# The fifth chunk of the keys in six batches: nine full-array products replaced by fifteen block products in column halves of TensorE

## The chip, the cores and the metric

One core of a Trainium2 chip. The metric is the device time of one execution, in microseconds, as the median of several runs. The engines are TensorE (PE in the profile, its weight loads PEld), VectorE (DVE), ScalarE (ACT), GpSimd (POOL) and SyncE (SP, which issues DMAs here). Each engine runs its own instructions in order and waits for the others at semaphores.

## The reference

Cross attention in 16 batches. x has 100 rows of 640 a batch; the context has 718 text rows and 4 token rows of 384; 8 heads of 80.

```python
query = hidden_states @ Wq
keyt = enc @ Wk
valt = enc @ Wv
hs = _mha(query, keyt, valt)                  # softmax(q k^T / sqrt(80)) v
ca_q1 = einsum('btc,th->bch', ca, Wq_ca)[:, indices, :]
ca_hs1 = _mha(ca_q1, residual, residual)      # the tokens' first attention
ca_q2 = ca_hs1 @ Wq
ca_hs2 = _mha(ca_q2, ca @ Wk_ca, ca @ Wv_ca)  # and their second, over 4 tokens
out = (hs + ca_hs2) @ Wout + b_out + residual
```

All in fp32. The change touches `keyt`: 718 rows x 384 times 384 x 640, in every batch.

## The kernel before

**Fast products.** The products enc·Wk and enc·Wv are 3x3 by 3x2 block products: the context in thirds of its rows (u, KT = 240 columns each, two halves of KN = 120) and thirds of its 384 channels (c), the weights in thirds of the channels and two column groups (g). Plainly that takes 18 block products. `V_PLAN` (L95) lists 15: each entry is a bank ("A" to "E"), a form f (a sum of blocks of the context times a sum of blocks of the weights) and the output (u, g) that is to receive the bank's running sum after this product. A bank is not cleared between its products, so what it holds must be read before its next product writes. `enc_sums` (L481) makes the context's forms on POOL, `weight_sums` (L502) the weights', once at the start.

**Keys in five chunks.** kT has five chunks of 128 columns of Wk. The first four go through `Keys` (L453) as two pairs (a pair is a chunk's two groups g) with 15 forms each, K_PLAN (L113), banks A and B in `psumk` tiles and C, D, E in `psum1`. The fifth has no partner: `last_keys` (L685) does it plainly in `chunk_keys` (L662) with nine products of 128x128 weights and 240 columns, the raw blocks of `wk4` against the raw context, and two ACT copies (L678).

**PSUM.** Eight banks in three rings of two: `pair` (two banks each), `psumk`, `psum1`. A tile taken from a ring has the place of the tile two before it and waits until that one's last reader is done.

**One batch b**, in the order of the program from L1353: scores of b in three parts (L695; the second in `psumk` and `psum1`, the others in pairs), copied by ACT into st[0..2]; the column maximum (`larger`, `most`, `top`, class `Maximum` L785: DVE transpose, maximum, small maxima, spread, transpose back); `subtract(i)` on DVE and `exponential(i)` on ACT for the three parts; all the while TensorE does `Values(b)` and `Keys(b + 1)` in small steps (`vv.go`, `kk.go`); then `last_keys(b + 1)`, for some batches the output projection of two row chunks (`project_pair`, L1144), for odd b the queries of the next two batches; last the weighted values, `a_ps` (L1589), in two groups of four heads, and for the next but one batch `second_next.products()` (y_ps).

From L1352 on the order on every engine is that of the program (`manual_schedule`). So an instruction that waits holds up everything behind it on its engine.

**Odd batches from 3 to 13** make the queries in `Queries.make` (L607), products of 128x64 weights and 100 columns in the two column halves of TensorE (k = 0 and 64, partitions 0 and 64 of the output), after one plain product for qz with 200 columns. Its weights' and queries' sums are made on POOL (`sums`, L578), in the part of the next enc tile that is still free. `project_pair` falls in the batches where `last.b` = b − 1 is in `PAIRS` = {2, 5, 7, 10, 12}: so in 3, 11 and 13 among the odd ones. In 5, 7 and 9 (`parted`) the last token's product in `values2` (L991, POOL) stands behind the sums.

**The tokens' attention** of the next batch (`second`, class `Second` L854): `scores1` on POOL, `softmax1` (a second `Maximum`) on DVE, `exponentials1` on ACT; the products `z_ps` (L931) that use it come after the next batch's scores. `values2` makes hs2 on POOL, which DVE adds to hs after each group of `a_ps` (L1610). `keys(m_next)` (L842) writes the masks for `y_ps`, also on POOL.

Of the kernel before, what the change touches and what calls it, by code (L numbers as in the profile page):

```python
# [8 lines left out]
F32 = mybir.dt.float32  # L9
# [112 lines left out]
W_AT |= {f: 6 + i for i, f in enumerate((0, 1, 2, 6, 10, 11, 12, 3, 13))}  # L122
NF = len(V_PLAN)


@with_exitstack
def kernel(
# [124 lines left out]
    wk_sb = const.tile([P, NF, 2, P], F32, name="wk_sb")  # L252
    wk4 = const.tile([P, CC, P], F32, name="wk4")
    wq_sb = const.tile([P, HC, H], F32, name="wq_sb")
    kT = const.tile([P, HC, 3, KT], F32, name="kT")
# [100 lines left out]

    most = const.tile([P, ROWS], F32, name="most")
    nc.gpsimd.memset(most[96:, :], LOW)

# [121 lines left out]
    def enc_sums(enc):  # L481
# [3 lines left out]
        for out, left, right, op in (  # L485
# [14 lines left out]
            nc.gpsimd.tensor_tensor(out, left, right, op)  # L500

    def weight_sums(engine, w, late=None, there={}):  # L502


        at = lambda f: there.get(f, w[:, W_AT[f]])
        raw = lambda c, g: w[:, 2 * (c - 1) + g - 1]
        for f, left, right in (
            (0, raw(1, 2), raw(1, 1)),
            (11, raw(2, 2), raw(3, 2)),
            (12, raw(3, 2), raw(3, 1)),  # L510
            (5, raw(2, 2), raw(1, 2)),
            (7, raw(3, 2), at(5)),
            (13, raw(3, 1), at(7)),
            (1, raw(2, 1), raw(3, 1)),
            (3, raw(1, 1), at(7)),
            (6, raw(2, 1), raw(1, 1)),
            (10, raw(3, 1), raw(2, 2)),
            (2, raw(1, 1), raw(2, 2)),
            (14, raw(2, 1), raw(2, 2)),
        ):  # L520
# [38 lines left out]
    class Queries:  # L559
# [46 lines left out]

        def make(self, tiles, between):  # L607
            qp, qz = tiles
# [12 lines left out]
            def add(bank, g, m):  # L621
                nc.vector.tensor_tensor(q(g, m), full(bank), q(g, m), ALU.add)

            for ch in range(HC):
                for k in (0, 64):
                    nc.tensor.matmul(
                        full(f)[k : k + 64],
                        wq_sb[:, ch, 4 * P + k : 4 * P + k + 64],
                        self.xT[:, :, ch, :],
                        start=(ch == 0),  # L630
                        stop=(ch == HC - 1),
                        skip_group_check=True,
                    )
# [51 lines left out]
    def last_keys(b, enc):  # L685
# [6 lines left out]
        )  # L692


    def scores(b, g, tiles):  # L695
# [89 lines left out]
    class Maximum:  # L785


        def __init__(self, top, name, scalar=False):

            self.name, self.scalar = name, scalar  # L790
            self.step = self.steps(top)
            self.over = None
# [5 lines left out]
        def steps(self, top):  # L798
# [6 lines left out]
            for j in range(4):  # L805
                nc.vector.tensor_reduce(
                    side[:, j, :], quad[32 * j : 32 * j + 32, :].unsqueeze(2), AX.X, ALU.max
                )
            mx = small.tile([P, NB], F32, tag="mx", name=f"mx_{name}")
            scalar = self.scalar  # L810
            rows = 64 if scalar else 32
            for lo in range(0, 64 if scalar else P, 32):
# [5 lines left out]
                )  # L818
            yield
            spread = wide(f"spread_{name}").rearrange("p (b k) -> p b k", k=32)  # L820
# [33 lines left out]
    class Second:  # L854


        def __init__(self, b, xT, ca=None):
            self.b, self.xT = b, xT[:, b % 2]
            self.top = None
# [35 lines left out]
        def scores1(self, behind=None, tokens=range(T)):  # L895
            b, g = self.b, self.g
            e = e1[:S].rearrange("p (h s) -> p h s", h=NH)
            for t in tokens:
# [9 lines left out]
                if t:  # L908
                    nc.gpsimd.tensor_tensor(e, e, to, ALU.add)  # L909
                elif behind:  # L910
                    wait_for(first, behind)

        def softmax1(self, n=8):

            if not self.top:
                self.top = Maximum(e1, f"1_{self.b}", self.b - 2 in PAIRS)
            if self.top.over is not None:
                return
            self.top.go(n)
            if self.top.over is not None:  # L920
                nc.vector.tensor_tensor(e1[:S], e1[:S], self.top.over[:S], ALU.subtract)

# [99 lines left out]
    class Last:  # L1022
# [120 lines left out]

        def project_pair(self):  # L1144

# [27 lines left out]

            product(b1, [(one[:, :2], w(0, 0))], True)
            read(b1, 0, 0)
            product(b2, [(one[:, 2:4], w(1, 0)), (one[:, 4:], last(0))], True)
            read(b2, 0, 0)
# [3 lines left out]
            nc.gpsimd.tensor_tensor(two[:, :2], two[:, 2:4], two[:, :2], less)  # L1181
            nc.gpsimd.tensor_tensor(wout2[:, 0], wout2[:, 0], w(0, 0), less)
            product(b4, [(two[:, 2:4], wout2[:, 1])], True)
            product(b1, [(sum1, w(0, 1))], False)
# [168 lines left out]
    for b in range(B):  # L1353
# [38 lines left out]
        if b == 0:  # L1392
            enc_sums(enc)
            now.load(nc.gpsimd)
            now.softmax1()
        st.append(scores(b, 0, tiles))
        if b == 0:
# [46 lines left out]
        elif b + 1 < B:  # L1444
# [36 lines left out]
            if last.b in PAIRS:  # L1481
                last.sums()
            parted = b % 2 and b > 1 and last.b not in PAIRS
            now.values2(None, range(T - 1 if parted else T))
            vv.go(2)
# [15 lines left out]
            mixed = None  # L1501
            if b % 2 and b > 1:
                second_next, enc_next = loads()
                mixed = Queries(p + 1, xT_at[0], enc_next[0])
            if parted:
                mixed.sums()
                now.values2(None, range(T - 1, T))
            if b == 1:
# [12 lines left out]
            if last.b in PAIRS:  # L1521
                second.softmax1(3)
                last.project_pair()
                if last.b == max(PAIRS):
# [3 lines left out]
                    )  # L1528
            second.softmax1(3 if parted else 8)
        else:  # L1530
# [26 lines left out]
        if b % 2 and b + 1 < B:  # L1557
            xT, tiles = xT_at[0], queries_tiles(p + 1)
            if not mixed:
                for n in range(HC):  # L1560
                    queries(p + 1, xT, tiles, n)
            elif parted:
                mixed.make(tiles, second.softmax1)
            else:
                keys(m_next)
                mixed.sums()
                mixed.make(tiles, second.softmax1)
        if 0 < b < B - 2:
            if not mixed or parted:
                keys(m_next)  # L1570
            enc_sums(enc_next)
        if 0 < b < B - 1:
            second.exponentials1()

        mine.hs = hs = hs_sb
        hs2 = now.hs2
        for g in range(2):
# [6 lines left out]
            for h, i in order:  # L1584
                if b == B - 1 and h == NH - 1 and i == 0:
# [91 lines left out]
```

## Time and profile before

| what | value |
|---|---|
| median of 3 runs | 917.0 us (916.76 to 918.83) |
| the profiled execution, its own time | 916.04 us |
| its span, first to last instruction | 914.1 us |
| granted TensorE clock | 1.0 of full speed |
| DVE, ACT, POOL busy | 699.0, 434.2, 706.8 us |
| SP's hardware queue | 59.18 MB, 21.2% of 16 engines' span |

The page's chain of waits goes back from the last instruction, at each step to what released it. A row of a group reads: line, engine, operation, output and inputs by name, shapes, count, then busy time, mean ns of one, and the engine's idle time before them. For TensorE a shape 128\*64 128x200 is: 128 rows by 64 columns of weights, 200 columns streamed. An fp32 product is two records, and its modelled length overlaps the next; the spacing of the starts is what it takes. A row of the timeline is start and length (us), engine, line, operation, names, shape, count, and in brackets the idle time before it with what ended it. A row of the waits is who waited, for whom, total us, times, longest.

### The profile page before, as it was taken

Reading aid. Unit: us, or ns where it says so; the run is one execution under the profiler, and the core shown is the slowest. Engines: PE = TensorE matmul, PEld = TensorE weight load, DVE = VectorE, ACT = ScalarE, POOL = GpSimd, SP = SyncE. Lnnn points to the kernel's source line nnn. Section 1 sums busy time; section 2 is a strip of 40 time slices with the busy share of each in tenths; the row PEclk is TensorE's granted clock in tenths of the full one; section 3 lists DMA queues with packets and bytes.
Section 4 is the critical chain, followed back from the end, with each engine's and each line's share of the span. In section 5 each row is a group of like instructions: output and inputs, shape, how many; then the busy total and the mean of one; then the engine's idle time right before and its main releaser. Section 6 shows DMA issues by size and latency. Waiting matters only on the chain.

```text
span 914.1 us, 27711 instructions
## 1 busy us (share of the span) xinstructions
PE 908.2 (99%) x11962; PEld 762.8 (83%) x11962; DVE 699.0 (76%) x1126; ACT 434.2 (47%) x834; POOL 706.8 (77%) x672
## 2 busy tenths in 40 slices
PE   9999999999999999999999999999999999999998
PEld 6988889797797979888798787988879788797866
DVE  3669795989759897785967869679785897748883
ACT  2244543736337363652727436274741737427341
POOL 8577999787958879696896959958797697976623
PEclk9999999999999999999999999999999999999999
DMA  8822111131301212130121301103120031210111
GB/s 269 294 75 63 47 47 53 37 94 52 96 18 50 80 38 69 55 104 32 51 56 54 105 32 52 55 25 105 54 82 32 25 106 53 82 46 24 61 45 39
DMA packets 50582, 62.94 MB, mean 69 GB/s; under 512 B 13682, under 2 KB 37810, under 8 KB 50460
## 3 DMA queue, kind: packets, MB, share of 16 engines
q1 hardware_dynamic: 48812, 59.18, 21.2%
q8 instruction: 94, 1.54, 0.7%
q10 hardware_dynamic: 1024, 1.15, 0.4%
q0 software_dynamic: 624, 0.85, 0.3%
q14 instruction: 28, 0.23, 0.1%
HBM read 55.59 MB, written 5.57 MB: 67 GB/s over the span
## 4 chain that ended last, share of the span: by engine, by line
PE 96%; DVE 3%; ACT 0%; issue 0%; DVEq 0%
PE a_ps L1589 12%; PE s_ps L710 12%; PE v_psA L434 11%; PE v_psB L434 9%; PE k_psA L465 8%; PE k_psB L465 7%; PE kT_ps L667 6%; PE o_ps L1161 5%; PE v_psC L434 4%; PE k_psC L465 3%; PE q_ps L594 2%; PE q_ps L536 2%; PE v_psE L434 2%; PE v_psD L434 2%; PE v_ps L375 2%; PE q_psA L594 1%
## 5 line engine op out<-in xcount | busy, mean ns | idle before, releaser
L902 POOL TENSOR_TENSOR e<-ca,g 100x800 f32<-100x800 f32 x64 | 99.3, 1562 | 107.0 <-ACT kT L407 78.5
L500 POOL TENSOR_TENSOR enc<-enc 128x240 f32<-128x240 f32 x144 | 113.3, 797 | 14.7 <-DMA enc<-in_enct 7.5
L1375 DVE TENSOR_TENSOR st<-st,over 120x1600 f32<-120x1600 f32 x48 | 114.9, 2395 | 0.0
L1589 PEld LDWEIGHTS a_ps<-vs,st 120*36 120x36 f32 (+3 forms) x3072 | 109.3, 124 | 3.5 <-issue 3.4
L1589 PE MATMUL a_ps<-vs,st 120*36 120x81 f32 (+3 forms) x3072 | 111.7, 233 | 0.0
L434 PE MATMUL v_psA<-wv_sb,enc 128*120 128x320 f32 x352 | 109.3, 433 | 0.0
L1008 POOL TENSOR_TENSOR hs<-hs,hs 100x640 f32<-100x640 f32 x48 | 94.8, 1974 | 3.8
L1001 POOL TENSOR_TENSOR hs<-vb,p 100x640 f32<-100x640 f32 x64 | 91.1, 1434 | 8.4 <-issue 4.7
L465 PE MATMUL k_psA<-enc,wk_sb 128*128 128x240 f32 x384 | 95.3, 371 | 0.1
L909 POOL TENSOR_TENSOR e<-e,e 100x800 f32<-100x800 f32 x48 | 91.8, 1913 | 3.8
L434 PE MATMUL v_psB<-wv_sb,enc 128*120 128x320 f32 x296 | 91.8, 433 | 0.0
L1383 ACT ACTIVATE st<-st 120x1600 f32<-120x1600 f32 x48 | 73.9, 1539 | 32.3 <-DVE st L1375 31.8
L465 PEld LDWEIGHTS k_psA<-enc,wk_sb 128*128 128x128 f32 x384 | 71.5, 190 | 16.3 <-DVE wk_sb L522 0.5
L434 PEld LDWEIGHTS v_psA<-wv_sb,enc 128*120 128x120 f32 x352 | 64.2, 183 | 25.0 <-DVE vs L405 0.5
L1387 DVE TENSOR_TENSOR most<-most,st 120x800 f32<-120x800 f32 x64 | 66.3, 1036 | 15.9 <-ACT st L760 14.7
L465 PE MATMUL k_psB<-enc,wk_sb 128*128 128x240 f32 x320 | 78.0, 366 | 0.3 <-DVE sm L983 0.3
L710 PE MATMUL s_ps<-qp,kT 64*56 64x100 f32 (+1 forms) x3072 | 73.1, 248 | 0.0
L434 PEld LDWEIGHTS v_psB<-wv_sb,enc 128*120 128x120 f32 x296 | 54.1, 183 | 21.9 <-DVE vs L405 0.4
L710 PEld LDWEIGHTS s_ps<-qp,kT 64*56 64x56 f32 (+1 forms) x3072 | 66.9, 130 | 5.4 <-issue 4.2
L1076 ACT COPY hsT<-turned_hs 32x160 f32<-32x160 f32 (+7 forms) x244 | 67.7, 277 | 3.0
L465 PEld LDWEIGHTS k_psB<-enc,wk_sb 128*128 128x128 f32 x320 | 60.7, 190 | 8.6 <-issue 0.7
L766 ACT COPY st<-s_ps 120x800 f32<-120x800 f32 x64 | 49.8, 829 | 33.6 <-PE s_ps L710 33.6
(196 smaller groups left out, 1824.6 us busy)
## 6 DMA issues: line engine op xcount, KB each, us to landing
vb<-va_d SPq DMA_DIRECT2D x62, 250.0 KB
enc<-in_enct SPq DMA_DIRECT2D x30, 240.0 KB
enc<-in_enct SPq DMA_DIRECT2D x15, 360.0 KB
xT<-in_xt SPq DMA_DIRECT2D x8, 500.0 KB
rest<-in_enct SPq DMA_DIRECT2D x31, 120.0 KB
xn<-in_x SPq DMA_DIRECT2D x11, 320.0 KB
out<-xn SPq DMA_DIRECT2D x11, 320.0 KB
ca<-in_cas SPq DMA_DIRECT2D x16, 156.2 KB
```

Source lines behind the costliest of these rows:

```text
L434: nc.tensor.matmul(at[0][j][:KN, : H // 2], a_form(self.enc, f)[:, j * KN : (j + 1) * KN], wv_there.get(f, wv_sb[:, W_AT[f]]), start=first ...
L465: nc.tensor.matmul(at[:, i * KT : (i + 1) * KT], wk_sb[:, W_AT[f], i], a_form(self.enc, f), start=(first and i == 0), stop=last, skip_grou ...
L500: nc.gpsimd.tensor_tensor(out, left, right, op)
L710: nc.tensor.matmul(s_ps[at][k0:k1, cols], w, rhs, start=not begun & {(at, k) for k in range(k0, k1, 32)}, stop=last, skip_group_check=True,)
L902: first = nc.gpsimd.tensor_tensor(to, self.ca[:, t, :].unsqueeze(1).to_broadcast([S, NH, S]), g[:, :, t].unsqueeze(2).to_broadcast([S, NH, ...
L909: nc.gpsimd.tensor_tensor(e, e, to, ALU.add)
L1001: first = nc.gpsimd.tensor_tensor(to, self.vb[t][:S].rearrange("p (h d) -> p h d", h=NH), p2[:, :, t].unsqueeze(2).to_broadcast([S, NH, D] ...
L1008: nc.gpsimd.tensor_tensor(sums, sums, to, ALU.add)
L1076: nc.scalar.copy(self.hsT(r)[32 * m : 32 * m + 32, :, first - lo : end - lo], turned[32 * i : 32 * i + 32, :, m, first - at : end - at],)
L1375: return nc.vector.tensor_tensor(st[i], st[i], top.over[:KN].unsqueeze(1).to_broadcast([KN, 2, ROWS]), ALU.subtract,)
L1383: nc.scalar.activation(st[i], st[i], AF.Exp, scale=SCALE)
L1589: nc.tensor.matmul(a_v[lo:hi, h % 4], st[i // 2][: KEYS[i], i % 2, h * S + lo : h * S + hi], block(i, h // 4)[: KEYS[i], h % 4], start=(i ...
```

## The change

In the batches of `MIXED` (b = 3, 5, 7, 9, 11, 13) `last_keys(b + 1)` is gone, and a class `Chunk` makes the fifth chunk of b + 1 from the 15 forms. Here the chunk's two groups g are its two column halves, 64 wide, and a product's output goes to partitions 0 to 63 or 64 to 127 of one of two `psum1` tiles: `one` holds bank A below and B above; `two` holds E below and C above, and bank D beside them, whose 240 columns are split in two halves of 120, one below and one above. `K4_PLAN` has eight steps: each names one or two products and what is read afterwards. A first read of an output is an ACT copy, a later one a DVE add; "AB" reads A and B for both groups in one instruction.

- `make` runs two steps ahead of the qz products, and one each after qz, after the first query bank's products, and after e's. Three more stand in `a_ps`: in group 0 before its 7th and 19th head-block, in group 1 before its 7th.
- `a_ps` of these batches takes `psumk` tiles instead of `psum1`, the two taken in reversed order.
- `w4_sums` (12 forms of 64 columns) is new; its sums are made by `weight_sums(nc.gpsimd, wk4)` at the start, behind the tokens' products of `scores1`. For its room, `most` is no longer a constant tile but one of the `wide` ring in each batch, whose rows 96 to 127 an ACT copy of `low` fills every time.
- In 5, 7 and 9 (`late`) `subtract(2)` and `exponential(2)` move into `make`, behind the qz products and behind the first query copy; the subtraction of the tokens' maximum and `exponentials1` move into `a_ps` (before its 19th head-block).
- In all six the last token's `values2` moves behind the `w2` subtraction in `make`; in 3, 11 and 13 `keys(m_next)` moves behind `make`, and `softmax1` runs in small steps between the reads of `project_pair`. `Maximum` has a `fine` mode with more steps.

```diff
+MIXED = range(3, B - 1, 2)
+K4_PLAN = [
+    ([("A", 7), ("B", 13)], [("A", (2, 1)), ("B", (1, 0))]),
+    ([("D", 1)], [("D", (2, 0))]),
+    ([("E", 6), ("B", 8)], [("B", (2, 0)), ("E", (1, 0))]),
+    ([("A", 3), ("B", 10)], [("AB", (2, None))]),
+    ([("A", 9), ("C", 12)], [("A", (1, 0))]),
+    ([("A", 2), ("B", 4)], [("AB", (0, None)), ("C", (0, 1))]),
+    ([("A", 0), ("B", 14)], [("A", (0, 1)), ("B", (0, 0))]),
+    ([("A", 5), ("C", 11)], [("A", (1, 1)), ("C", (2, 1))]),
+]
...
-    most = const.tile([P, ROWS], F32, name="most")
-    nc.gpsimd.memset(most[96:, :], LOW)
+    low = const.tile([P, 1], F32, name="low")
+    nc.gpsimd.memset(low, LOW)
...
+            chunk.go(2)
             for ch in range(HC):
...
             for u in range(2):
                 nc.scalar.mul(
                     qz[:, 0, :, u * S : (u + 1) * S], full(f), qmask[:, u : u + 1]
                 )
+            between(2)
+            steps[0]()
+            chunk.go()
             self.product(a, w(0, 0), v(0, 0), True)
             nc.scalar.copy(q(0, 0), full(a))
+            steps[1]()
             self.rest(c, 0, 0, True)
             self.product(c, w(0, 1), v(1, 0), False)
             add(c, 0, 0)
+            chunk.go()
+            between(1)
             self.product(a, self.w2, self.t2, False)
             nc.gpsimd.tensor_tensor(self.w2, w(0, 1), self.w2, ALU.subtract)
+            steps[2]()
             self.rest(e, 1, 0, True)
+            between(1)
             self.product(e, w(1, 1), self.t4, False)
             nc.scalar.copy(q(1, 0), full(e))
             add(a, 1, 0)
+            chunk.go()
             self.product(b, self.w3, self.t3, True)
             add(b, 1, 0)
+            between(1)
...
+    class Chunk:
+        def __init__(self, b, enc):
+            self.enc = enc
+            one, two = psum1(f"k4_psA_{b}"), psum1(f"k4_psC_{b}")
+            half = P // 2
+            self.at = {
+                "A": [(one, 0, 0, 0, KT)],
+                "B": [(one, half, 0, 0, KT)],
+                "C": [(two, half, 0, 0, KT)],
+                "D": [(two, i * half, KT, i * KN, KN) for i in range(2)],
+                "E": [(two, 0, 0, 0, KT)],
+            }
+            self.one = one
+            self.plan = iter(K4_PLAN)
+            self.opened, self.begun = set(), set()
+
+        def move(self, out, left, at):
+            if at <= self.begun:
+                nc.vector.tensor_tensor(out, left, out, ALU.add)
+            else:
+                nc.scalar.copy(out, left)
+            self.begun |= at
+
+        def go(self, n=1):
+            half = P // 2
+            for _, (products, reads) in zip(range(n), self.plan):
+                for bank, f in products:
+                    for tile, k, lo, c0, w in self.at[bank]:
+                        nc.tensor.matmul(
+                            tile[k : k + half, lo : lo + w],
+                            w4_form(f),
+                            a_form(self.enc, f)[:, c0 : c0 + w],
+                            start=bank not in self.opened,
+                            stop=True,
+                            skip_group_check=True,
+                        )
+                    self.opened.add(bank)
...
-    second.scores1()
+    made = second.scores1()
+    with tc.issue_after(made.ins):
+        weight_sums(nc.gpsimd, wk4)
...
+        most = wide(f"most_{b}")
+        nc.scalar.copy(most[96:], low[96:].to_broadcast([P - 96, ROWS]))
...
-            subtract(2)
-            exponential(2)
-            last_keys(b + 1, enc)
+            late = mixed and last.b not in PAIRS
+            if not late:
+                subtract(2)
+                exponential(2)
+            if not mixed:
+                last_keys(b + 1, enc)
...
-                second.softmax1(3)
-                last.project_pair()
+                if not mixed:
+                    second.softmax1(3)
+                last.project_pair(second.softmax1 if mixed else lambda n: None)
...
             else:
-                keys(m_next)
-                mixed.sums()
-                mixed.make(tiles, second.softmax1)
+                if last.b in PAIRS:
+                    second.softmax1()
+                    mixed.sums()
+                chunk = Chunk(b + 1, enc)
+                mixed.make(
+                    tiles,
+                    chunk,
+                    lambda n=9: second.softmax1(n, True),
+                    (
+                        lambda: late and subtract(2),
+                        lambda: late and exponential(2),
+                        lambda: now.values2(None, later),
+                    ),
+                )
...
+        a_pss = [psumk(f"a_ps_{b}_{g}") for g in (1, 0)][::-1] if mixed else None
         for g in range(2):
-            a_ps = psum1(f"a_ps_{b}_{g}")
+            a_ps = a_pss[g] if mixed else psum1(f"a_ps_{b}_{g}")
...
+                if mixed and (g, n) in ((0, 6), (0, 18), (1, 6)):
+                    chunk.go()
+                    if held and (g, n) == (0, 18):
+                        second.softmax1()
+                        second.exponentials1()
```

More of the change, by code (lines that the diff above doesn't have):

```diff
@@ L605, in rest, with make @@
             self.product(bank, weights, self.xT[:, m, 4:], first)
-        def make(self, tiles, between):
+        def make(self, tiles, chunk, between, steps):
             qp, qz = tiles
@@ L896, in scores1 @@
             b, g = self.b, self.g
+            made = None
             e = e1[:S].rearrange("p (h s) -> p h s", h=NH)
@@ L1482 @@
                 last.sums()
-            parted = b % 2 and b > 1 and last.b not in PAIRS
-            now.values2(None, range(T - 1 if parted else T))
+            later = range(T - 1, T) if b in MIXED else range(0)
+            now.values2(None, range(T - len(later)))
             vv.go(2)
@@ L1501 @@
             mixed = None
-            if b % 2 and b > 1:
+            if b in MIXED:
                 second_next, enc_next = loads()
                 mixed = Queries(p + 1, xT_at[0], enc_next[0])
-            if parted:
-                mixed.sums()
-                now.values2(None, range(T - 1, T))
+                if last.b not in PAIRS:
+                    mixed.sums()
             if b == 1:
@@ L1528 @@
                     )
-            second.softmax1(3 if parted else 8)
+            if not mixed:
+                second.softmax1(8)
         else:
@@ L1561 @@
                     queries(p + 1, xT, tiles, n)
-            elif parted:
-                mixed.make(tiles, second.softmax1)
-            else:
-                keys(m_next)
-                mixed.sums()
-                mixed.make(tiles, second.softmax1)
+            else:
+                if last.b in PAIRS:
+                    second.softmax1()
+                    mixed.sums()
+                chunk = Chunk(b + 1, enc)
[8 more added lines that the diff above has]
+                    ),
+                )
         if 0 < b < B - 2:
-            if not mixed or parted:
-                keys(m_next)
+            keys(m_next)
             enc_sums(enc_next)
-        if 0 < b < B - 1:
+        held = b in MIXED and not second.less
+        if 0 < b < B - 1 and not held:
             second.exponentials1()
```

60 lines of the change are left out of this document (48 added, 12 removed).

## The prediction, made blind

> **What bounds the kernel now.** I read the page first (busy times, the chain that ended last), then the waits of TensorE, then stretches of the timeline in the batches that change.
>
> ```profile
> span 914.1 us, 27711 instructions
> PE 908.2 (99%) x11962; PEld 762.8 (83%) x11962; DVE 699.0 (76%) x1126; ACT 434.2 (47%) x834; POOL 706.8 (77%) x672
> PE 96%; DVE 3%; ACT 0%; issue 0%; DVEq 0%
> ```
> ```profile
> PE idle_ps L1227 <- DVE idle L1224: 1.1, 1, 1.1
> PE m_ps L1262 <- issue: 0.5, 1, 0.5
> PE k_psB L465 <- DVE sm L983: 0.3, 1, 0.3
> ```
>
> TensorE works 908.2 of 914.1 us and is 96% of the chain. All its waits in the whole run are the three rows of the second fence, 1.9 us, none of them in batches 3 to 13. So the time is a sum of TensorE streams. A change gains what it takes out of that sum, and loses every wait that it opens in a stream that has none.
>
> **What the removed products cost.** The change replaces `last_keys` in batches 3, 5, 7, 9, 11 and 13. Here is batch 3 in the chain of waits, and batch 5 on TensorE's timeline (start, length, line, shape, count):
>
> ```profile
> 236.50 3.65 PE kT_ps L667 x18
> ```
> ```profile
> 348.74 1.38 PE L667 MATMUL kT_ps<-enc,wk 128*128 128x240 f32 x6
> ...
> 352.48 1.91 PE L626 MATMUL q_ps<-xT,wq_sb 128*64 128x200 f32 x20
> 354.22 0.86 PE L594 MATMUL q_psA<-xT,wq_sb 128*64 128x100 f32 x16
> 354.90 1.20 PE L594 MATMUL q_ps<-xT,wq_sb 128*64 128x100 f32 x24
> ...
> 360.40 6.94 PE L1589 MATMUL a_ps<-vs,st 120*64 120x81 f32 x192
> ...
> 369.54 1.63 PE L710 MATMUL s_ps<-qz,kT 32*120 32x200 f32 x32
> 374.88 0.75 PE L931 MATMUL z_ps<-y_sb,e 100*32 100x33 f32 x64
> ```
>
> Nine fp32 products are 18 records, two passes each: 3.65/18 = 0.203 us for a pass of 240 columns over the full array. Six batches: 21.9 us leave TensorE.
>
> **What the added products cost.** Eight steps. Seven hold two products of 128x64 weights with 240 columns, one in the left column half and one in the right; one (form 1, bank D) streams its two halves of 120 columns side by side. The question is whether two halves with different streams run at once. The trace has one such place, `project_few` in batch 15:
>
> ```profile
> 874.11 1.24 PE L434 MATMUL v_psD<-wv_sb,enc 128*120 128x320 f32 x4
> 875.28 2.91 PE L1207 MATMUL o_ps<-wout_sb,hsT 128*64 128x320 f32 x20
> 878.12 1.07 PE L434 MATMUL v_psA<-wv_sb,enc 128*120 128x320 f32 x3
> ```
>
> Twenty passes of 320 columns, in two column halves with different streams, take 878.12 − 875.28 = 2.84 us, 0.284 us a pair with the start of the mode in it. The four passes of 320 columns over the full array ahead of them take 1.17, 0.29 each: a pair costs what one full pass costs. The query products above say the same: 16 passes of 100 columns in 354.90 − 354.22 = 0.68 us, 0.085 a pair. I take a pair at the price of one full pass. The chunk is then 7 × 2 × 0.203 + 2 × 0.102 = 3.05 us (0.102 is half of 0.203; the 0.085 of 100 columns and 0.203 are its bounds). Saved: 0.60 a batch, 3.6 in all.
>
> [...]
>
> Not shown by the trace: what a lone visit of a 240-column pair costs among narrow streams (six steps stand alone, between query products or in `a_ps`). Lower bound 0: the step from 200 to 100 columns at 354.22 loses nothing. Upper bound: one stream idles while the other finishes, 0.203 − 0.085 = 0.12 a visit, 6 × 6 × 0.12 = 4.3 us. I take 0, since the nearest row is that step.
>
> **The wait that opens in batches 3, 11 and 13.** There `project_pair` now comes straight behind the last products of `Keys`. Before, the nine products stood between. Its first bank is `b1`, the first of two `psumk` tiles: the ring has two, four are taken ahead of it in the batch (two by the scores, then k_psA and k_psB), so `b1` gets k_psA's place. K_PLAN ends with bank A, whose last read is an ACT copy:
>
> ```profile
> 235.52 0.97 PE L465 MATMUL k_psA<-enc,wk_sb 128*128 128x240 f32 x4
> 236.33 1.38 PE L667 MATMUL kT_ps<-enc,wk 128*128 128x240 f32 x6
> 239.98 2.85 PE L1161 MATMUL o_ps<-wout_sb,hsT 128*128 128x320 f32 x10
> ```
> ```profile
> 236.53 0.56 ACT L407 COPY kT<-k_psA 128x480 f32<-128x480 f32 x1
> ```
>
> TensorE is free at 236.33, the copy ends at 237.09, and its release takes some 0.06 (my estimate; in the waits above PE never waited for ACT, and the next ACT instruction, at 237.19, is 0.10 behind the copy): a stall of 0.82 us where there was none. Bounds: 0 if the ring falls otherwise, 1.0 if the copy starts 0.2 later. I take 0.82, three times: 2.5 us. In 5, 7 and 9 the chunk itself follows k_psA, in `psum1` banks whose last reader is the DVE add of k_psC at 347.05 (below); it needn't wait.
>
> **What is hidden, batch 5 (7 and 9 alike).** DVE, ACT:
>
> ```profile
> 347.05 0.66 DVE L405 TENSOR_TENSOR kT<-k_psC,kT 128x480 f32<-128x480 f32 x1
> 349.36 1.01 DVE L801 STREAM_TRANSPOSE turned<-e 128x800 f32<-128x800 f32 x1
> 350.40 0.99 DVE L803 TENSOR_REDUCE quad<-turned 128x25 f32<-128x800 f32 x1
> 356.22 0.37 DVE L622 TENSOR_TENSOR qp<-q_ps,qp 128x200 f32<-128x200 f32 x1 [2.72 <-PE q_ps L594]
> ```
> ```profile
> L1375 DVE TENSOR_TENSOR st<-st,over 120x1600 f32<-120x1600 f32 x48 | 114.9, 2395 | 0.0
> ```
> ```profile
> 349.54 1.54 ACT L1383 ACTIVATE st<-st 120x1600 f32<-120x1600 f32 x1
> ```
>
> A chunk is read by 6 ACT copies and 8 DVE adds in place of two copies. From 200 columns in 0.37 and 480 in 0.66 an add of 240 is some 0.4, so 3.3 us more of DVE a batch, and 1 to 2 of ACT; DVE idles 2.72 at 356.22 alone. The tightest step is the fourth, which writes bank B that DVE must have read. DVE now does transpose, maximum, `subtract(2)` and then the read: 347.71 + 1.01 + 0.99 + 2.40 + 0.4 and four gaps of 0.03 = 352.6. TensorE reaches step four at 348.74 + 0.61 (steps one, two) + 1.74 (qz) + 0.41 + 0.68 (product a) + 1.03 (24 passes at 0.085 a pair) = 353.2. Slack 0.6. `exponential(2)` comes behind the copy of product a, which is out at 352.2: 0.2, 0.33 and 1.54 on, near 354.3 instead of 351.1. Its reader is the last third of `a_ps` g=0, past 360: hidden by 6 us. The tokens' exponential of 5, 7 and 9 and the chunk's last reads come in the middle of `a_ps`, near 365 and 366; their readers are the products at 374.88 and at 369.54. In batch 3 DVE goes from the pair's reads through these to the same read:
>
> ```profile
> 249.87 0.89 DVE L1172 TENSOR_TENSOR xn<-o_ps,xn 128x320 f32<-128x320 f32 x2 [0.59 <-PE o_ps L1161]
> 250.68 1.00 DVE L831 STREAM_TRANSPOSE over<-spread 128x800 f32<-128x800 f32 x1
> 251.71 1.64 DVE L921 TENSOR_TENSOR e<-e,over 100x800 f32<-100x800 f32 x1
> ```
>
> ```profile
> 249.76 1.91 PE L626 MATMUL q_ps<-xT,wq_sb 128*64 128x200 f32 x20
> ```
>
> The three end at 253.35 and the read at 253.8. That is batch 3 as it was; all of it moves up with TensorE, whose fourth step, with the first one in the place of the qz products, would stand at 249.76 + 0.61 + 1.74 + 0.41 + 0.68 + 1.03 = 254.2 on the same scale. Slack 0.4.
>
> `a_ps` now lies in `psumk`. Its first group waits for the ACT copy of q_psB, one product (0.69) behind, as tight as 0.1 us; the copy before took 0.33 and ACT has nothing else there. On POOL:
>
> ```profile
> L846 POOL TENSOR_TENSOR m<-mb,hmask 128x64 f32<-128x64 f32 x42 | 13.1, 313 | 6.6 <-DMA mb<-m_d 6.6
> ```
> ```profile
> L1008 POOL TENSOR_TENSOR hs<-hs,hs 100x640 f32<-100x640 f32 x48 | 94.8, 1974 | 3.8
> L1001 POOL TENSOR_TENSOR hs<-vb,p 100x640 f32<-100x640 f32 x64 | 91.1, 1434 | 8.4 <-issue 4.7
> ```
> ```profile
> POOL e L902 <- ACT kT L407: 78.5, 10, 9.7
> ```
> ```profile
> 54.49 0.69 POOL L500 TENSOR_TENSOR enc<-enc 128x240 f32<-128x240 f32 x1 [5.64 <-DMA enc<-in_enct]
> ```
>
> The last token's two instructions (1.43 + 1.97) go behind the `w2` subtraction, past which no DMA moves (token 3 issues none); in 3, 11 and 13 `keys(m_next)`, five masks of about 0.31, goes behind `make`. Their readers, the DVE adds of hs2 and the `y_ps` products, come behind the halves of `a_ps` (6.94 us). The `enc_sums` end up to 3.4 later, and POOL then idles before the next tokens' products, up to 9.7 us in ten batches. On SP the load of `rest` no longer waits for products, so it lands sooner. The twelve weight sums at the start, near 0.31 each, 3.8 us, fit the idle 5.64.
>
> The sixteen ACT copies of `low` (32x800; a 64x800 copy takes 0.86, so less) go between `y_sb` and the first scores copy, where ACT idles 1.15 us, and 0.54 where it is worst:
>
> ```profile
> 370.58 1.55 ACT L766 COPY st<-s_ps 120x800 f32<-120x800 f32 x2 [1.15 <-PE s_ps L710]
> ...
> 267.87 1.55 ACT L766 COPY st<-s_ps 120x800 f32<-120x800 f32 x2 [0.54 <-PE s_ps L710]
> ...
> 240.89 1.73 ACT L823 COPY spread<-mx 64x800 f32<-64x800 f32 x2
> ```
>
> The excess of 0.32 at most delays copies whose banks TensorE wants again some 0.4 later: 0.
>
> **The sum.** −3.6 + 2.5 = −1.1 us. Batches 5, 7 and 9 gain 0.60 each, batches 3, 11 and 13 lose 0.22 each. The profiled execution took 916.04 us (span 914.1 and 1.9 around it), so 914.9; the median of the runs is 917.0, 0.96 above it, so 915.9. With the stall at its bounds and small waits of 0 to 0.5: 915.2 to 917.0.
>
> **Rivals.**
> First, no wait in 3, 11, 13. The full 3.6 comes out: 913.4. For it: TensorE has hardly a wait anywhere, so banks may fall otherwise than I count. Against: the rows at 236.33 and 236.53 put the copy 0.76 past the point where the bank is wanted. 0.22.
>
> Second, slower: the chunk's reads come late. Each step overwrites what ACT or DVE has yet to read, and the fourth has only 0.4 to 0.6 us of slack behind DVE's long subtraction. `subtract(2)` varies; with DVE 1.5 us later, 0.9 to 1.1 are waited for in each of the six, +6, and 917.0 − 1.1 + 6 = 921.9; lone visits at their upper bound give 920.2. It decides from 0.2 us a batch beyond the slack (1.1/6). Against it: DVE's idle 2.72. [...] 0.23.
>
> Third, the change doesn't do what it says: the two column halves run one after the other. 7 × 4 × 0.203 + 4 × 0.102 = 6.1 us in place of 3.65, 2.4 × 6 = 14.7 more and 2.5 of stalls: 934. Against it stands the row at 875.28. 0.05.
>
> **How the numbers follow.** My forecast has 0.50, the rivals 0.22, 0.23 and 0.05. Faster by over 0.3% means under 914.25, which is the first rival and a rim of mine: 0.25. Slower by over 0.3%, above 919.75 (0.3% is about what a measurement of this kernel can tell), is most of the second and the third: 0.23. The rest, 0.52, is within. The range takes in the first rival's 913.4 and the second's up to 920.0: 913.2 to 920.0.
>
> **What would show it.** Right: chunk passes start in pairs, about 0.2 us apart for 240 columns; TensorE's waits gain three of about 0.8 us at `project_pair`'s first product, released by ACT's kT copy; no others at L465's successors, in `make` or `a_ps`. Wrong: no such wait; waits released by DVE's kT adds; or steps of more than 0.41 us with no wait named.

## The result, and the profile after

The changed kernel takes 913.44 us (median of 6 runs, 912.76 to 914.68); the kernel before took 917.24 us in 6 runs beside it. The ratio is 0.9958, 95% interval 0.9945 to 0.997: 3.8 us or 0.42% faster, and the interval lies wholly below 1. The time lies in the predicted range and at its low end: it is the first rival's 913.4, not the forecast's 915.9. (The spans of the two profiled executions, 914.1 and 911.6 us, differ by 2.5 only; the six runs after spread by 1.9.)

The page of the profile after: span, TensorE's busy row, and the chain that ended last.

```profile
span 911.6 us, 28003 instructions
...
PE 904.9 (99%) x12046; PEld 755.5 (83%) x12046; DVE 719.5 (79%) x1174; ACT 455.0 (50%) x874; POOL 711.5 (78%) x684
...
PE 96%; DVE 2%; DMA 0%; ACT 0%; issue 0%; ACTq 0%; DVEq 0%
```

TensorE's waits after (who waited for whom, total us, times, longest):

```profile
PE idle_ps L1330 <- DVE idle L1327: 1.1, 1, 1.1
PE m_ps L1365 <- issue: 0.5, 1, 0.5
PE k_psB L481 <- DVE sm L1083: 0.3, 1, 0.3
PE z_ps L1031 <- issue: 0.2, 1, 0.2
PE v_ps L391 <- DMA wv_sb<-in_wv: 0.2, 1, 0.2
```

TensorE is still a sum without gaps, and none of the three waits of 0.8 us that the forecast put into batches 3, 11 and 13 is there. DVE has 20.5 us more work than before and ACT 20.8, and none of it shows: no row names the chunk (L760 here) or `project_pair` (L1261).

Batch 3 (up to 251.16) and step four in batch 5 (352.73) on TensorE's timeline. The spacing of the starts is what a row takes:

```profile
235.68 0.97 PE L481 MATMUL k_psA<-enc,wk_sb 128*128 128x240 f32 x4
236.49 2.85 PE L1261 MATMUL o_ps<-wout_sb,hsT 128*128 128x320 f32 x10
239.19 1.24 PE L1261 MATMUL o_ps<-wout,hsT 128*128 128x320 f32 x4
...
246.28 0.63 PE L760 MATMUL k_psA<-enc,w_sums 128*64 128x240 f32 x4
246.73 0.38 PE L760 MATMUL k_psC<-enc,w_sums 128*64 128x120 f32 x4
246.94 1.86 PE L651 MATMUL q_ps<-xT,wq_sb 128*64 128x200 f32 x20
248.63 0.37 PE L760 MATMUL k_psC<-enc,w_sums 128*64 128x240 f32 x1
248.64 0.37 PE L760 MATMUL k_psA<-enc,wk 128*64 128x240 f32 x1
248.83 0.37 PE L760 MATMUL k_psC<-enc,w_sums 128*64 128x240 f32 x1
248.84 0.37 PE L760 MATMUL k_psA<-enc,wk 128*64 128x240 f32 x1
249.03 0.86 PE L618 MATMUL q_psA<-xT,wq_sb 128*64 128x100 f32 x16
...
250.75 0.57 PE L760 MATMUL k_psA<-enc,w_sums 128*64 128x240 f32 x4
251.16 0.86 PE L618 MATMUL q_psA<-enc 128*64 128x100 f32 x16
...
352.73 0.58 PE L760 MATMUL k_psA<-enc,w_sums 128*64 128x240 f32 x4
```

The passes start in pairs 0.01 us apart (248.63 and 248.64) and a pair every 0.20 (248.83): two halves with different streams run side by side. Step three takes 249.03 − 248.63 = 0.40 us, the lone step four 251.16 − 250.75 = 0.41, the split form 0.21, the first step 0.45 with the start of the mode (the passage from full-array to half-array products) in it. The other four steps take 0.40 or 0.41 each. The eight add to 3.10 against 3.65, and with the mode's start, which the queries no longer pay (the qz products take 1.69 us now and took 1.74 before), each of the six batches is 0.60 shorter.

ACT's copy of k_psA in batch 3, for which the forecast made `b1` wait:

```profile
236.69 0.56 ACT L423 COPY kT<-k_psA 128x480 f32<-128x480 f32 x1
```

It runs until 237.25, and `project_pair` starts at 236.49 all the same. So `b1` does not stand in k_psA's place.

DVE's read ahead of step four, batch 3 and batch 5:

```profile
249.32 0.41 DVE L750 TENSOR_TENSOR kT<-k_psA,kT 64x240 f32<-64x240 f32 x1
...
351.85 0.41 DVE L750 TENSOR_TENSOR kT<-k_psA,kT 64x240 f32<-64x240 f32 x1
```

They end at 249.73 and 352.26. TensorE comes to step four at 250.75 and 352.73: the slack is 1.02 us in batch 3 and 0.47 in batch 5.

### The profile page after: what moved, and what is told of

The parts are those of the page before. It is cut to its first block, busy times and chain, and to the rows that moved or that the text cites. A ratio compares the mean times of both kernels' runs of the same rounds, so it can differ in the third digit from the quotient of the medians.

```text
span 911.6 us, 28003 instructions
## 1 busy us (share of the span) xinstructions
PE 904.9 (99%) x12046; PEld 755.5 (83%) x12046; DVE 719.5 (79%) x1174; ACT 455.0 (50%) x874; POOL 711.5 (78%) x684
## 3 DMA queue, kind: packets, MB, share of 16 engines
q10 hardware_dynamic: 1024, 1.15, 0.4%
## 4 chain that ended last, share of the span: by engine, by line
PE 96%; DVE 2%; DMA 0%; ACT 0%; issue 0%; ACTq 0%; DVEq 0%
PE a_ps L1716 12%; PE s_ps L799 12%; PE v_psA L450 11%; PE v_psB L450 9%; PE k_psA L481 9%; PE k_psB L481 7%; PE o_ps L1261 5%; PE kT_ps L702 4%; PE v_psC L450 4%; PE k_psC L481 3%; PE q_ps L618 2%; PE q_ps L560 2%; PE v_psD L450 2%; PE v_psE L450 2%; PE k_psA L760 2%; PE v_ps L391 1%
## 5 line engine op out<-in xcount | busy, mean ns | idle before, releaser
L1480 DVE TENSOR_TENSOR st<-st,over 120x1600 f32<-120x1600 f32 x48 | 119.0, 2482 | 0.0
L1716 PEld LDWEIGHTS a_ps<-vs,st 120*36 120x36 f32 (+3 forms) x3072 | 111.7, 125 | 5.8 <-issue 3.4
L1716 PE MATMUL a_ps<-vs,st 120*36 120x81 f32 (+3 forms) x3072 | 114.7, 233 | 0.0
L799 PE MATMUL s_ps<-qp,kT 64*64 64x100 f32 (+1 forms) x3072 | 73.1, 248 | 0.0
L799 PEld LDWEIGHTS s_ps<-qp,kT 64*64 64x64 f32 (+1 forms) x3072 | 66.9, 130 | 5.4 <-issue 4.2
L423 ACT COPY vs<-v_psA 120x640 f32<-120x640 f32 x45 | 31.2, 693 | 65.1 <-PE v_psA L450 64.9
```

Of the source, the lines that this page charges most:

```text
L799: nc.tensor.matmul(s_ps[at][k0:k1, cols], w, rhs, start=not begun & {(at, k) for k in range(k0, k1, 32)}, stop=last, skip_group_check=True,)
L1480: return nc.vector.tensor_tensor(st[i], st[i], top.over[:KN].unsqueeze(1).to_broadcast([KN, 2, ROWS]), ALU.subtract,)
L1716: nc.tensor.matmul(a_v[lo:hi, h % 4], st[i // 2][: KEYS[i], i % 2, h * S + lo : h * S + hi], block(i, h // 4)[: KEYS[i], h % 4], start=(i ...
```

## The experiments

Edits are against the kernel after. Each run's ratio is to the kernel before on the same chip; the kernel after stands at 0.9958.

**The moves without the new products.** The nine plain products go back to their place, everything that was moved stays moved.

```diff
-            if not mixed:
-                last_keys(b + 1, enc)
+            last_keys(b + 1, enc)
...
-            self.plan = iter(K4_PLAN)
+            self.plan = iter(())
```

> All of the change stays (weight sums, wide most, moved subtract(2), exponentials, last token, psumk for a_ps, small steps of softmax1), but in the six batches the nine plain products come back in their old place and the chunk does nothing. Theory: the whole gain is TensorE's streams, 3.65 against 3.05 to 3.1 a batch, and the moves are hidden: +3.3 to +3.6 on the span of 911.6, so 914.9 to 915.2. Rival: the moves of DVE, ACT and POOL work made part of the gain: then the span stays under 914.

Measured: 918.13 us, ratio 0.9999 (0.9989 to 1.0009). The gain is gone, so it is that of the shorter streams; the weight sums behind the tokens' products, the exponential put off and `a_ps` in other banks give and cost nothing beyond 0.1%.

**Which accumulator, which place.** First the names of the two accumulators were exchanged:

```diff
             b1, b2 = psumk(f"o_ps1_{r}"), psumk(f"o_ps2_{r}")
+            if self.b + 1 in MIXED:
+                b1, b2 = b2, b1
```

> In 3, 11 and 13 the two banks of project_pair are exchanged, so that b1 lies where k_psA was (bank 4 of PSUM in batch 3; in the changed kernel b1 has bank 5, k_psB's place). Theory: the changed kernel has no wait there only because b1 fell into k_psB's place, and my price of the wait was right: TensorE waits for ACT's kT copy (end 237.25 against 236.49 in batch 3 of the changed kernel, and 0.06 to release), 0.8 us in each of three batches, span 911.6 + 2.5 = 914.1. Rival: the copy is no obstacle wherever b1 lies: span 911.6 within 0.5 and no wait of TensorE at project_pair.

Measured: 913.66 us, ratio 0.9955 (0.9939 to 0.9972), and no wait at `project_pair`. This edit did not change what it was meant to change: in the PSUM addresses of the compiled kernel the accumulator used first has k_psB's bank again (bank 5 in batch 3; k_psA has 4), whatever its name.

The same happened with the order in which the two `a_ps` tiles are taken:

```diff
-        a_pss = [psumk(f"a_ps_{b}_{g}") for g in (1, 0)][::-1] if mixed else None
+        a_pss = [psumk(f"a_ps_{b}_{g}") for g in (0, 1)] if mixed else None
```

> The two psumk tiles of a_ps are taken in plain order, so that group 0 gets q_psA's place instead of q_psB's. Theory: group 0 then waits for DVE's last two query adds: in batch 3 of the changed kernel they end at 256.95 and a_ps starts at 256.02, in batch 5 359.80 and 358.01: with 0.06 to release 1.0 us in each of 3, 11, 13 and 1.85 in each of 5, 7, 9, +8.5 on the span (920). Rival: places are not decisive here, group 0's first products don't wait: within 0.5 of 911.6.

Measured: 913.48 us, ratio 0.9953 (0.9938 to 0.9968); in the compiled kernel the first group's tile kept q_psB's bank (5 in batch 3). So in both a place went by first use, not by the order of taking as the section on the kernel before has it, and the next edit changed the first use:

```diff
+            if self.b + 1 in MIXED:
+                nc.tensor.matmul(b2[:, : H // 2], one[:, 0], w(0, 0)[:, 0],
+                                 start=True, stop=True, skip_group_check=True)
             product(b1, [(one[:, :2], w(0, 0))], True)
```

> In project_pair of batches 3, 11 and 13 one plain product of 320 columns goes into the second accumulator ahead of the first one's (the second is started afresh behind it, so nothing of it stays). The accumulator used first then stands in the place of k_psB, and the first accumulator in that of k_psA, whose read by ScalarE ends 0.76 us after the pair's start in the trace of after. Theory (the predicted wait is real but hung on which place an accumulator gets): TensorE is held for about 0.5 us at the second product of each pair, released by ScalarE's kT copy; with 0.2 us for the added product this is 3 x 0.75 = 2.2 us, 915.7. Rival (the place makes no difference, the copy is not waited for): only the added products, 3 x 0.2 = 0.6 us, 914.0, and no wait named.

Measured: 917.93 us, ratio 0.9992 (0.9981 to 1.0003), span 914.7 against 911.6. Batch 3, TensorE (L1275 is the added product):

```profile
236.96 0.70 PE L1275 MATMUL o_ps<-wout_sb,hsT 128*128 128x320 f32 x2
237.77 2.96 PE L1261 MATMUL o_ps<-wout_sb,hsT 128*128 128x320 f32 x10
```

ACT's copy in that run, and what the products of L1261 sat idle for (us, times):

```profile
237.16 0.56 ACT L423 COPY kT<-k_psA 128x480 f32<-128x480 f32 x1
```
```profile
  ACT kT L423: 1.9, 3
```

Now `b1` waits for ACT's copy of k_psA, in exactly three places. Its first product starts 237.77 − 236.96 = 0.81 us behind the pair's start and 0.05 behind the copy's end at 237.72. The added product covers part of it: its two passes cost 2 × 0.27 (ten take 239.19 − 236.49 = 2.70 in the kernel after; the expectation's 0.2 was too small). From the starts, the pair is 0.92 us longer in each of the three batches. So the predicted wait, 0.82, is there, within a hundredth, once the accumulator has k_psA's place. Three of 0.81, with the 0.1 that the first pass behind a wait is longer, are 2.7 us; the kernel after plus 2.7 is 916.2, near the forecast's 915.9.

**DVE's slack ahead of step four.** One extra DVE maximum of 120x800 (`over` with itself, which changes nothing) ahead of the chunk's reads, then two, then one and a half:

```diff
             steps[0]()
+            for _ in range(1):   # or 2; the third run: one and a half
+                steps[3]()
             chunk.go()
```

> One more VectorE operation of 120x800 (about 1.05 us by the rows of most) ahead of the chunk's reads in each of the six batches. Theory (VectorE's reads have a slack of about 0.4 us ahead of step four in batches 5, 7 and 9 and about 0.95 in 3, 11 and 13): 3 x 0.65 + 3 x 0.1 = 2.3 us, 915.7, as waits of the chunk's product for VectorE's kT add. Rival (the reads have several us of slack, the prediction's second rival was far off): no change, 913.4.

> Two such operations, 2.1 us. Theory: 3 x 1.7 + 3 x 1.15 = 8.5 us, 922.0, waits of the chunk's product for VectorE's kT add, one of 1 to 2 us in each batch; if such a wait also lowers the granted clock, some us more. Rival: no change, 913.4.

> Between the runs with one and with two extra VectorE operations: one of 120x800 and one of 120x400 ahead of the chunk's reads. In batches 5, 7 and 9 the wait at step four should then be about 1.4 us (0.73 with one, 2.05 with two, where the clock fell to half behind it), in 3, 11 and 13 about 0.3. Theory A (a wait of some 2 us is needed before the clock falls): 3 x 1.4 + 3 x 0.3 = 5.1 us more than after, span 916.7, clock 1.0 throughout. Theory B (1.4 us of idle is enough): some 1.7 us more in each of 5, 7 and 9, span 922, and a granted clock of about 0.5 for 3 to 4 us behind step four.

Measured: one, 917.88 us, ratio 0.9993 (0.9979 to 1.0006), span 916.0; one and a half, 921.7, 1.0052 (1.0035 to 1.0068), span 919.5; two, 928.69, 1.0112 (1.0089 to 1.0136), span 929.0. TensorE's wait row with one, with one and a half and with two:

```profile
PE k_psA L762 <- DVE kT L752: 2.2, 3, 0.7
```
```profile
PE k_psA L762 <- DVE kT L752: 6.2, 6, 1.6
```
```profile
PE k_psA L762 <- DVE kT L752: 8.7, 6, 2.0
```

One operation opens three waits of 0.73 us, in 5, 7 and 9 alone; batches 3, 11 and 13 swallow it. That is the theory's pattern. The sizes are off because the added operation isn't 1.05 us everywhere. DVE with two of them, batch 3 and batch 5:

```profile
251.33 2.02 DVE L1688 TENSOR_TENSOR over<-over 120x800 f32<-120x800 f32 x2
...
355.24 2.61 DVE L1688 TENSOR_TENSOR over<-over 120x800 f32<-120x800 f32 x2
```

They take 1.01 each in batch 3 and 1.31 in batch 5, with the gaps between. With one of 1.29 in batch 5 and 0.73 waited for, the slack is some 0.56; with 2.02 in batch 3 and 0.85 waited for ((8.7 − 3 × 2.05)/3, 2.05 being the wait of batch 5), some 1.2. With two, batches 5, 7 and 9 lose 3.7 to 4.1 us each for waits of about 2; the rest is the clock. Stretches of that run: us, busy us and count of PE, PEld, DVE, ACT, POOL, then the granted clock, the DMA share and GB/s:

```profile
250.00:254.00 4.00, 3.16 (x58) 2.72 (x55) 3.83 (x6) 1.34 (x5) 0.00 (x0) 1.00 0.21 82
...
354.00:358.30 4.30, 2.30 (x48) 1.98 (x42) 4.19 (x4) 2.51 (x4) 4.30 (x3) 1.00 0.63 177
...
355.48:358.89 3.41, 1.36 (x27) 1.05 (x24) 3.31 (x5) 1.60 (x2) 3.41 (x3) 1.00 0.31 80
358.89:362.30 3.41, 3.41 (x44) 3.40 (x42) 1.72 (x8) 0.00 (x0) 1.97 (x3) 0.50 0.03 5
```

Behind the wait of 2.05 us (batch 5, until 358.35) the clock is half for 3.41 us, with TensorE busy throughout. That costs 1.7 more. The run with one and a half speaks against theory B of its expectation: its waits, 1.63 us in batch 5 and 1.64 in batch 7, leave the clock as it was, and its mean over the run is 0.999. Batch 7, with the wait in the first row:

```profile
467.39:470.80 3.41, 1.77 (x36) 1.46 (x34) 3.27 (x8) 1.34 (x1) 2.83 (x2) 1.00 0.21 61
470.80:474.20 3.40, 3.40 (x80) 3.28 (x76) 2.82 (x11) 0.43 (x2) 3.07 (x3) 1.00 0.02 5
```

Its span is still 7.9 us above the kernel after's, for 6.2 us of waits. A row of the waits understates each by some 0.2 us, because the modelled length of the record ahead runs past the next start: from the starts the wait of batch 5 costs 1.85, not 1.63. Three of 1.85 and three of 0.65 make 7.5.

**All eight steps at once**, at the start of `make`, with nothing between a step and the reads it waits for:

```diff
-            chunk.go(2)
+            chunk.go(len(K4_PLAN))
```

> All eight steps of the chunk stand together at the start of make. Theory: a step's read costs a round trip of 0.2 (PE's end to the read) + 0.36 to 0.41 (the read) + 0.06, and only the work between the steps hides it: about 0.65 a step for seven steps less what follows in other banks, some 4 us a batch, +24 in all (16 to 32), as TensorE's waits for DVE and ACT kT reads. Rival: DVE and ACT are ahead of TensorE and a read costs TensorE next to nothing: under +5.

Measured: 964.56 us, ratio 1.0517 (1.0494 to 1.0539), span 962.8, mean clock 0.975. The waits:

```profile
PE k_psA L760 <- DVE kT L750: 15.8, 24, 0.9
PE k_psC L760 <- ACT kT L752: 6.9, 6, 1.1
PE k_psA L760 <- ACT kT L752: 2.7, 6, 0.5
```

They are 25.4 us, but the span grew by 51.2. Stretches of batch 3, columns as above:

```profile
248.51:251.92 3.41, 1.88 (x12) 0.59 (x12) 2.31 (x5) 0.12 (x1) 0.00 (x0) 1.00 0.24 96
251.92:255.33 3.41, 2.13 (x8) 0.59 (x8) 1.12 (x3) 0.36 (x1) 0.00 (x0) 0.50 0.00 0
255.33:258.75 3.42, 2.85 (x16) 1.95 (x18) 0.91 (x3) 0.35 (x1) 0.00 (x0) 0.50 0.00 0
```

No wait of batch 3 is longer than 1.15 us, yet after 3.41 us with TensorE busy for 1.88 the clock falls to half, for 6.83 us. TensorE is busy for 2.13 + 2.85 = 4.98 of these, so half speed costs 2.5. The six waits of the batch add to 4.4 by their rows and, with 0.2 more for each, to 5.6. Both together are about the 8.0 us by which the batch is longer than in the kernel after.

**More batches.** Could the exchange be made elsewhere? In batches 6 and 8 (with `project_pair`) and in 2, 4, 10, 12 and 14 (without) the chunk's steps went between the products of `a_ps`, and `a_ps`, `softmax1` and `exponentials1` moved as in the six:

```diff
+MORE = (6, 8)            # the second run: (2, 4, 10, 12, 14)
...
-            if not mixed:
+            if not (mixed or b in MORE):
                 last_keys(b + 1, enc)
...
+                if b in MORE:
+                    # the second run: (0, 10), (0, 14), (0, 19) for (0, 6), (0, 12), (0, 18)
+                    chunk.go({(0, 0): 2, (0, 6): 1, (0, 12): 1, (0, 18): 1,
+                              (1, 0): 1, (1, 6): 1, (1, 15): 1}.get((g, n), 0))
```

> The block products also in batches 6 and 8, where project_pair stands ahead of the weight sums: all eight steps go between the products of a_ps, and the weight sums and the exponential move as in the six. Theory (each batch saves 0.60 us of streams and the reads are hidden): 2 x 0.6 = 1.2 us less, 912.2, span 910.4. Rival (VectorE's or ScalarE's reads come late, with a_ps's own reads in front of them): waits of 0.5 to 1.5 us in each, 913.2 to 915.2.

> The block products also in batches 2, 4, 10, 12 and 14, where no project_pair stands; all eight steps go between the products of a_ps, step three behind 10 of its block pairs, so that ScalarE's two copies are done by then; the weight sums and exponential1 move as in the run with 6 and 8. Theory (each batch changes 3.65 us of plain streams for 3.1 to 3.2 of chunk, and the reads are hidden): 5 x 0.5 = 2.5 us less than after's 911.6 us of span, 909.1, ratio to before 0.993. Rival (the earlier keys of the next batch were cover for other work, as the weight sums were for GpSimd's w_out sums in batches 6 and 8): waits of 0.5 to 1.0 us that take the gain back, span 911 to 914, ratio 0.995 to 0.998.

Measured: 6 and 8, 917.02 us, ratio 0.9992 (0.9979 to 1.0005), span 916.0. The five others, 951.65, ratio 1.0367 (1.0351 to 1.0382), span 947.5, mean clock 0.981. In 6 and 8 two waits appear that the kernel after hasn't:

```profile
PE o_ps L1262 <- POOL wout L1285: 0.8, 2, 0.4
PE k_psC L761 <- ACT kT L753: 0.6, 2, 0.3
```

The chunk saves 0.45 a batch there (3.20 for 3.65, from the starts), `project_pair` loses 1.0 and `a_ps` 0.54. POOL makes the difference of w_out for the pair's last product; the nine plain products, 3.65 us of TensorE ahead of the pair, had covered that (two of the expectations call them the weight sums). That is 1.1 us more a batch, 2.2 of the 4.4 by which the span grew. The other 2.2 us lie in TensorE's start (1.1, with a wait of 0.9 for the weights' DMA) and mostly in `z_ps` of batches 11 and 13, outside the edit.

In the five, the chunk's steps wait for the two readers:

```profile
PE k_psC L761 <- ACT kT L753: 11.9, 5, 2.4
PE k_psA L761 <- DVE kT L751: 11.7, 6, 2.4
```

What DVE does ahead of its first read in batch 4 of that run:

```profile
307.39 2.86 DVE L1481 TENSOR_TENSOR st<-st,over 120x1600 f32<-120x1600 f32 x1
...
315.35 1.01 DVE L926 STREAM_TRANSPOSE over<-spread 128x800 f32<-128x800 f32 x1
316.39 0.41 DVE L751 TENSOR_TENSOR kT<-k_psA,kT 64x240 f32<-64x240 f32 x1
```

This is nine microseconds of softmax work ahead of the read. In the kernel after, the 3.65 us of plain products and the undisturbed `a_ps` run beside it, and in the six batches of the change the queries' products stand there as cover. The rival holds, at a far larger size than it gave, since the clock fell as well, to 0.50 in the last row here. Batch 4, columns as above, where a wait of 2.38 us ends at 313.22 and one of 2.44 at 316.86:

```profile
308.24:311.65 3.41, 2.60 (x51) 2.00 (x49) 3.38 (x3) 2.21 (x3) 3.33 (x2) 1.00 0.71 203
311.65:315.07 3.42, 1.20 (x20) 0.90 (x20) 3.24 (x10) 1.45 (x5) 1.72 (x7) 1.00 0.53 145
315.07:318.48 3.41, 1.62 (x16) 1.29 (x18) 2.47 (x5) 0.00 (x0) 3.25 (x6) 0.50 0.00 0
```

Last, for 6 and 8, the first two steps as cover inside `project_pair`:

```diff
+            if chunk:
+                chunk.go()
             product(b1, [(one[:, 2:4], w(1, 1)), (one[:, 4:], last(1))], False)
             read(b1, 0, 1)
+            if chunk:
+                chunk.go()
             product(b3, [(two[:, :2], wout2[:, 0])], True)
```

> Batches 6 and 8 again, but the chunk's first step stands ahead of project_pair's product of b1 for the second part, and its second step ahead of b3's, the product that waited for GpSimd's w_out sum. Theory (in the run with 6 and 8 the weight sums had covered GpSimd's chain hsT, hsT, w_out, which then was late by 0.3 and 0.42 us, and ScalarE's copies were late by 0.3): the 0.46 and 0.2 us of the two steps take up these waits, the wait for ScalarE goes, and each batch is some 0.3 us shorter than in after: span 911.0, ratio to before 0.995. Rival (GpSimd's chain starts later by as much, or VectorE's reads come late): o_ps stays some 0.5 us longer or a new wait comes in the a_ps products, span 912 to 914.

Measured: 917.17 us, ratio 0.9981 (0.9972 to 0.9991). The waits for POOL are gone from the list, as they should be if cover was what lacked, but DVE is late instead, by up to 0.3:

```profile
PE k_psA L761 <- DVE kT L751: 1.1, 4, 0.3
```

The pair is now 0.40 longer than in the kernel after and `a_ps` 0.9: each batch is 1.1 us worse, as without the steps in the pair. No version here beats the kernel after.

## Why the prediction was right or wrong

- **The bound** was right: TensorE as a sum without gaps. The run with the plain products put back loses the gain, so the streams made it.
- **The price of the chunk** was right: 3.10 measured, 3.05 worked out; 0.60 saved a batch, 3.6 in six. The pairs cost what one full pass costs, 0.20. The steps take 0.40 to 0.41 us, the first 0.45. Lone visits cost nothing, the lower bound that was taken.
- **The failed step is "so `b1` gets k_psA's place"**, worked out by counting four tiles ahead in a ring of two. The profile before doesn't show which place a tile gets, and the count was taken as if it did. The compiled kernel before shows it: in batch 3 `b1` already has bank 5, k_psB's, and k_psA has 4. In the kernel after, too, the accumulator used first has the bank that is freed earlier, k_psB's. The wait's size, 0.82, was right: with the other accumulator used first it measured 0.81, with 0.05 between the copy's end and the product where the prediction estimated 0.06. This one step is the 2.5 us between the forecast and the result, and its lower bound, 0 "if the ring falls otherwise", is what happened: the prediction's own sign of being wrong, "no such wait". The range holds the result only because it took in the first rival. The forecast's own band, 915.2 to 917.0, doesn't: it is said to have the stall at its bounds, but with 0 the sum gives 913.4.
- **What is hidden** was right. The slack ahead of step four was worked out as 0.6 us in batch 5 and 0.4 in batch 3; the trace has 0.47 and 1.02. In batch 3 the subtraction on `e` took 0.99 us instead of the 1.64 counted. The moved work on POOL and ACT, the `low` copies and the first group of `a_ps` opened no wait.
- **The second rival** (late reads) was a live one: one more DVE operation of 1.0 to 1.3 us in the six batches takes the whole gain back (ratio 0.9993). Its price left out the clock, which with two such operations was 0.50 for 3.41 us behind the wait of batch 5.
- **The third rival** fell with the pairs 0.01 us apart.

The weight went wrong with the step: the first rival, which was given 0.22, had the same working as the forecast but for the place of one bank.

## What to carry to other kernels

Where TensorE is a gapless sum, price a change by the spacing of starts in its own streams, and then look for what the removed streams covered: the same exchange that gains 0.6 us a batch beside the queries loses where w_out's differences or the softmax stood behind those streams. Don't infer a PSUM wait by counting tiles of a ring; find the address in the compiled kernel, or give "no wait" and "wait" like chances. Price a wait on TensorE at its length only while it is short and alone: here single waits of 1.63 and 1.64 us left the clock at 1.00, but behind one of 2.05 it was 0.50 for 3.41 us, and among six of at most 1.15 for 6.83.

## What the runs showed of the hardware that was not expected

**Around some waits of TensorE the granted clock was 0.50 for a while, around others it stayed at 1.00.** In the run with two operations it was 0.50 for 3.41 us (358.89 to 362.30, batch 5), behind a wait of 2.05. With all steps at once it was 0.50 for 6.83 us (251.92 to 258.75, batch 3), among six waits of at most 1.15. With five more batches it was 1.00 in batch 4 until 315.07, past a wait of 2.38 that ended at 313.22, and 0.50 from there to 318.48, from within the next wait, of 2.44. With one and a half operations it stayed at 1.00 around 1.63 us of waiting in batch 5 and 1.64 in batch 7. In the rows above, TensorE sat idle for 2.05 of the 3.41 us ahead of the fall with two operations and for 1.53 of those ahead of the fall with all steps at once, but for 1.64 of 3.41 with one and a half, where the clock stayed. So neither the longest wait nor this idle time tells the cases apart; what does is not shown.

**The same DVE operation took 1.01 us in one place and 1.31 in another**: in the run with two of them POOL was busy for 0.00 us of the stretch from 250 to 254, where they took 1.01, and for all of 354.0 to 358.3, where they took 1.31. In the run with one, the one in batch 5 took 1.29. No run separated POOL from another cause: the DMA share differed as well, 0.21 and 0.63.

**Left open:** `z_ps` varies by up to 0.8 us between runs with waits that the profile names "issue", in batches that no edit touched.
